# Keeping transposed rows in DRAM, and transposing heads' results by blocks on VectorE

## The chip, the cores and the metric

One core of a Trainium2 chip runs the kernel. The metric is the device time of one execution in microseconds (us), measured by the host several times; one further execution was recorded by the hardware profiler. The engines are TensorE (PE; its weight loads are listed as PEld), VectorE (DVE), ScalarE (ACT), GpSimd (POOL) and SyncE (SP), which here does nothing but issue transfers (DMAs). Each engine works through its own instructions strictly in order.

## What is computed

A transformer block on x of 8 rows (batch) x 512 tokens x 128 features, all in float32. Attention and a mixture of experts both start from the normalized input, and both are added to x:

```python
xn = _layernorm(x)                                # over the 128 features
# attention: 8 heads; each head has two score maps of 8 features
scores = einsum('bqhif,bkhif->ibhqk', xn @ Wq.T, xn @ Wk.T) * 8**-0.5
atts = softmax(scores); att = atts[0] - diff_weight * atts[1]
o = einsum('bhqk,bkhe->bqhe', att, xn @ Wv.T)
normed = o * rsqrt(mean(o * o) + eps) * norm_w    # mean over all heads of a token
attn = (normed @ Wo.T + bo) * (1 - diff_weight)
# experts: one shared and 8 routed, two of them per token
gates = sigmoid(xn @ Wg); vals, idx = top_k(gates, 2); vals /= vals.sum()
shared = silu(xn @ Ws1) * (xn @ Ws3) @ Ws2
routed = sum of vals * (silu(xn @ We1[e]) * (xn @ We3[e]) @ We2[e]) over the two experts
x + attn + (shared + routed) / 3
```

## The kernel before

Tokens lie on the 128 partitions, four tiles of 128 tokens to a row of the batch (`NT = 4`). The attention is the backbone. A row has four pairs of heads (`w`), and each pair is done in four steps (`c`, 128 keys each): 16 steps to a row, 128 in all (`STEPS * B`), numbered 0 to 127 in this text. A step has two halves. Each half issues two score matmuls (`scores`, L807, tile `sc`, a PSUM buffer with no second copy) whose exponential ScalarE takes (`pe`, L815), and two matmuls `mx` with a VectorE reduction `most` (`maxima`, L758 and L765). The maxima are those of later heads, some six steps ahead; when a pair's are complete, `shift` turns them (VectorE transposes 128x32 into `rows`, a store to `turned` in DRAM, and half a step later a load into `qst`), so that the exponentials of that pair are safe. The second half of a step also weighs the values with the exponentials of the step before (`weigh`, L826, tile `av`).

All other work is cut into pieces, which are Python generators put on a list by `job(first, last, pieces, part, ready, kept_off)`. In the first half of each step `pieces` walks the list, ordered by `last` less the pieces left, and starts the next piece of every job that fits: a piece yields a pair of its estimated TensorE time and its PSUM banks, a step has room for 3.6 us (`ROOM`) and three banks. What a job does on TensorE is issued in the first half, after that half's scores and maxima; what follows a `yield "soon"` right after the pieces of that step, and what follows `yield "late"` in the second half. So the planner fixes the order of each engine's instructions when the kernel is built. A piece of cost zero takes no room.

The jobs that matter here:

- `gates_later`: for rows 1 to 7, one a step from step 4, transposes the normalized row (`turn`, four TensorE transposes `px` into PSUM, L246), copies it out as `xnT` on ScalarE (L283) and, a step later, multiplies it by the gate weights. The pool of `xnT` has three buffers, so a row's transposed form does not stay.
- `route`: sorts tokens to experts on VectorE in steps 11 to 19. Rows are then scattered to `slots` by GpSimd, one indirect transfer a half (L441).
- `prepare(b)`: some 16 steps ahead of row `b`, transposes the row again (L665, copy L667) unless `state[b]` holds it (rows 0 and 1), makes queries and keys (`pq`, L672) and values (`pv`, L716); the parts go to `qst` and `kst` by transfers on SP (`copies`).
- `shared_ahead(b)`: the shared expert of rows 1 to 7, steps 13 to 47; transposes the row a third time (L932, copy L934) where it is not held, then `ps` (L847), tanh and two VectorE products `th_s` and `h_s`, and `ph` (L864).
- `expert(q)`, 18 groups of four blocks from step 49, one every 3.95 steps: `pxq` (transposes, L543), `ph` (L567) twice, each with a tanh on ScalarE and VectorE's `th` (L531) and `h` (L534), then `py` (L580), which needs both `h`.
- `fold(b, w)`: transposes the weighed values of a pair of heads (`po`, L876); VectorE divides (`rec` L881, `on` L883), GpSimd subtracts the second map and writes `o` (L887).
- `conclude(b)`: when the four folds of a row are done, transposes its results `o` (`pn`, L899), takes them out of PSUM scaled by `nw_s` as `oT` (L902), squares and sums them on VectorE (`sq`, L907), raises to the power -1/2 on GpSimd (L910), multiplies by Wo (`pz`, L915) and adds to the residual (`r`, four VectorE operations, L919). `kept_off` keeps its pieces out of every fourth step.

`keep_busy` and `keep_clock` are matmuls whose result is not used; in steps 0 to 3 (`CATCH_UP`) a second tile of maxima is done per step, in two separate halves (L742, L749). SP's queue carries nearly all transfers in the order of issue.

Of the kernel before, what the change touches and what calls it, by code (L numbers as in the profile page):

```python
# [19 lines left out]
P = 128  # L20
# [11 lines left out]
def kernel(  # L32
# [209 lines left out]
    def turn(b):  # L242
# [4 lines left out]
        xnT = p3.tile([P, S], F32, tag="xnT", name=f"xnT_{b}")  # L247
        return xnT, px

    gated = []  # L250
    pgs = []

# [15 lines left out]
    def gates_later(rows):  # L268

        previous = None  # L270
        for b, ready_at in rows.items():
            while step < ready_at:
                yield 0, 0
            yield 1.35, 1
            if previous:
                gates(*previous)
            if b in state and "xnT" in state[b]:
                previous = b, state[b]["xnT"]
                continue
            xnT, px = turn(b)  # L280
            previous = b, xnT
            yield "late"
            nc.scalar.copy(xnT, px)  # L283
        yield 0.9, 0
        gates(*previous)
        yield "late"
        nc.scalar.activation(
            gate.rearrange("p t e -> p (t e)"), pgs[0][:, : TILES * NE], AF.Exp, scale=-1.0
        )
        held.pop()  # L290
        gated.append(True)
# [188 lines left out]
    def keep_expert(e):  # L480
# [6 lines left out]
            in_=We2[e].rearrange("(c p) d -> p c d", p=P),  # L487
        )

    def fetch(q):  # L490

        xq = p3.tile([P, QUAD, SENT], F32, tag="xq", name=f"xq_{q}")
        ws = []
        blocks[q] = xq, ws

        def take():
            nc.sync.dma_start(
                out=xq,
                in_=slots[q * QUAD * P : (q + 1) * QUAD * P, :].rearrange("(n p) e -> p n e", p=P),
            )  # L500
            landing.append(turns + 3)

        def load(n):
            w = p12.tile([P, WIDE], F32, tag="w", name=f"w_{q}_{n}")
            j = q * QUAD + n
            e = nc.values_load(
                expert_of[0:1, j : j + 1],
                engines=[mybir.EngineType.SP],
                min_val=0,
                max_val=NE - 1,  # L510
                skip_runtime_bounds_check_because="a count of NE - 1 comparisons",
            )
            nc.sync.dma_start(out=w, in_=experts[bass.ds(e * P, P), :])
            ws.append(w)
            if n == QUAD - 1:
                fetched.append(q)
                (loads if routed else waiting).append(take)

        yield 0, 0
        yield "late"  # L520
        for n in range(0, QUAD, 2):
            loads.append(lambda n=n: (load(n), load(n + 1)))
# [137 lines left out]
    def prepare(b):  # L660

        st = state[b]
        if "xnT" not in st:
            yield 0.45, 1
            st["xnT"], px = turn(b)  # L665
            yield "late"
            nc.scalar.copy(st["xnT"], px)  # L667
        xnT = st["xnT"]
        yield 1.75, 2
        pqs = [small_psum(f"pq_{b}_{i}") for i in range(2)]  # L670
        for i in range(2):
            nc.tensor.matmul(  # L672
                pqs[i],
                w_c[:, i].rearrange("p i f u -> p (i f u)") if b else w_rest[:, i],
                xnT,
                start=True,
                stop=True,
            )
        parts = []
        for i in range(2):  # L680
            yield ("soon", "late")[i]
            upper = p1.tile([P, S], F32R, tag=f"upper{i}", name=f"upper_{b}_{i}")
            nc.scalar.copy(upper, pqs[i])
            lower = p1.tile([P, S], F32R, tag=f"lower{i}", name=f"lower_{b}_{i}")
            nc.vector.tensor_tensor(lower, pqs[i], upper.bitcast(F32), ALU.subtract)
            parts.append((upper, lower))
        q, k = qst[b % 2], kst[b % 2]

        def no_shift():
            for half in range(2):  # L690
                nc.sync.dma_start(
                    out=q[64 * half + SHIFT : 64 * half + SHIFT + 2]
                    .bitcast(F32)
                    .rearrange("p u s -> p (u s)"),
                    in_=noughts,
                )

        def copy(part, i, s):

            row_of = (2 * part + s, part + 2 * s)[i]  # L700
            first = 0 if b else 2
            for half in range(2):
                (nc.scalar if b == 0 and i and part else nc.sync).dma_start(
                    out=(q, k)[i][64 * half + row_of : 64 * half + STACK : 4, first:, :].bitcast(F32),
                    in_=parts[i][part][64 * half : 64 * half + F * (H - first), :].bitcast(F32),
                )

        if b > 1:
            copies.append(no_shift)
        for part, i in ((0, 0), (0, 1), (1, 0), (1, 1)):  # L710
            for s in range(2):
                copies.append(lambda part=part, i=i, s=s: copy(part, i, s))
        yield 0.9, 1
        pv = small_psum(f"pv_{b}")
        for t in range(NT):
            nc.tensor.matmul(  # L716
                pv[:, t * P : (t + 1) * P],
                xnT[:, t * P : (t + 1) * P],
                w_t[:, 0, :],
                start=True,  # L720
                stop=True,
            )
        yield "late"
        nc.scalar.copy(
            vals[b % 2].rearrange("p t h e -> p (t h) e")[:, :, 0:DH],
            pv.rearrange("p (n e) -> p n e", e=DH),
        )
# [52 lines left out]
    def into_queries(b, w, rows):  # L780
        n = rows.shape[0]
        for i in range(2):
            (nc.sync if b or w else nc.scalar).dma_start(
                out=qst[b % 2][64 * i + SHIFT : 64 * i + SHIFT + 2, 2 * w : 2 * w + 2, :].bitcast(F32),
                in_=rows[n // 2 * i : n // 2 * (i + 1), :],
            )
# [80 lines left out]
    def fold(b, w):  # L867
# [21 lines left out]
        )  # L889
        st["folds"] = st.get("folds", 0) + 1  # L890

    def conclude(b):

        st = state[b]
        yield 0.45, 1
        o = st["o"].rearrange("p t h e -> p t (h e)")
        pn = small_psum(f"pn_{b}")
        for t in range(NT):
            nc.tensor.transpose(pn[:, t * P : (t + 1) * P], o[:, t, :], ident)  # L899
        yield "soon"  # L900
        oT = p1.tile([P, S], F32, tag="oT", name=f"oT_{b}")
        nc.scalar.activation(oT, pn, AF.Identity, scale=nw_s)  # L902
        yield "late"
        sq = p2.tile([P, 4 * NT, DH], F32, tag="on", name=f"sq_{b}").rearrange("p n e -> p (n e)")[:, :E]
        rms = p2.tile([P, NT], F32, tag="rms", name=f"rms_{b}")
        for t in range(NT):
            nc.vector.tensor_tensor_reduce(  # L907
                sq, o[:, t, :], o[:, t, :], 1.0 / E, RMS_EPS, ALU.mult, ALU.add, rms[:, t : t + 1]
            )
        nc.gpsimd.tensor_tensor(rms, rms, minus_half, ALU.pow)  # L910
        yield 0.9, 1
        pz = small_psum(f"pz_{b}")
        for t in range(NT):
            ts = slice(t * P, (t + 1) * P)
            nc.tensor.matmul(pz[:, ts], oT[:, ts], w_t[:, 1, :], start=True, stop=True)  # L915
        yield "late"
        r = st["r"]
        for t in range(NT):
            nc.vector.scalar_tensor_tensor(  # L919
                r[:, t, :], pz[:, t * P : (t + 1) * P], rms[:, t : t + 1], r[:, t, :], ALU.mult, ALU.add  # L920
            )
        settle(b)
# [4 lines left out]
    def shared_ahead(b):  # L927

        xnT = state[b].get("xnT")
        if xnT is None:  # L930
            yield 0.45, 1
            xnT, px = turn(b)  # L932
            yield "late"
            nc.scalar.copy(xnT, px)  # L934
        hs = yield from shared_up(b, xnT)
        yield 1.8, 1
        ph = shared_down(b, hs)
# [55 lines left out]
    for b in range(B):  # L993
        at = STEPS * b
        st = state[b]
        if b == 1:
            job(1, 2, 2, prepare(b))
        elif b > 1:
            job(at - 16, at - 15, 3, prepare(b))
        if b < AHEAD:  # L1000
            job(at + 5, at + 13, 2, shared(b), lambda b=b: len(over) == b)
            job(at + 12, at + 18, 1, shared_out(b), lambda st=st: "h" in st and "r" in st)
        else:
            n = int(13 + 5.3 * (b - AHEAD))
            job(n, n + 5, 4, shared_ahead(b), lambda b=b: len(done_ahead) == b - AHEAD)
        job(
            at + 3, at + 4, 1, residual(b), lambda b=b: len(rows_sent) >= b and (b < AHEAD or b in kept)
        )
        for w in range(4):
# [3 lines left out]
        job(  # L1013
            at + 17,
            at + 21,
            2,
            conclude(b),
            lambda st=st: st.get("folds") == 4 and "r" in st,
            kept_off=b < B - 1,
# [63 lines left out]
    with tc.manual_schedule():  # L1083
# [116 lines left out]
        nc.vector.tensor_scalar(keep, dw, -1.0, 1.0, ALU.mult, ALU.add)  # L1200
        nw_s = const.tile([P, 1], F32, name="nw_s")
        nc.vector.tensor_scalar(nw_s, nw, keep, None, ALU.mult)
        nc.gpsimd.tensor_scalar(bo_b, bo_b, keep, None, ALU.mult)
        nc.gpsimd.tensor_scalar(s2, s2, OUT_SCALE, None, ALU.mult)
        count_up()
# [39 lines left out]
        while step < total + 1 or jobs or errands or loads:  # L1245
            for second_half in range(2):
# [28 lines left out]
                else:  # L1275
                    follow(begun, "late")
                    if last is not None:
                        weigh(*last)
                    if turns in CATCH_UP:
                        apart.append(True)  # L1280
                        next_maxima(1)
                        apart.pop()
# [50 lines left out]
```

## Time and profile before

| | us |
|---|---|
| median of 9 runs | 664.42 |
| lowest and highest | 659.71, 668.34 |
| the profiled execution, as timed | 659.84 |
| its span, first to last instruction | 657.7 |
| busy in the span: PE, PEld | 604.4, 313.6 |
| busy in the span: DVE, ACT, POOL | 492.9, 362.9, 288.6 |

Busy time counts an engine's instructions and not the register or DMA-issuing ones. Overlapping matmuls are counted once in a group's busy time, so a group's busy time divided by its count is less than the mean duration of one. The mean granted TensorE clock was 0.986 of full speed. A line of the timeline has the start in us from the span's start, the duration, the engine and line, the operation with the tile it writes and the tiles it reads, and in brackets how long the engine was idle before it and what ended that.

### The profile page before, as it was taken

To read this page: it belongs to the slowest core of one execution; us is meant where nothing else is said; L and a number is where in the kernel's file an instruction comes from. 1 tells how busy PE (TensorE), PEld (TensorE's weight loads), DVE (VectorE), ACT (ScalarE), POOL (GpSimd) and SP (SyncE) were. 2 spreads that over 40 slices of the span, in tenths; PEclk is the share of its full clock that TensorE was granted. 3 is DMA by queue.
4 is the path that set the end of the run, shared out by engine and by line. 5 is a ranking of instruction groups with operands and counts; after the bars stand their busy time and mean duration, and the time that the engine had idled before them with its cause. 6 is when DMAs were issued, how large, how long until landed. Compare 5 with 4: busy or idle time off the path is not lost.

```text
span 657.7 us, 10907 instructions
## 1 busy us (share of the span) xinstructions
PE 604.4 (92%) x3725; PEld 313.6 (48%) x3725; DVE 492.9 (75%) x914; ACT 362.9 (55%) x447; POOL 288.6 (44%) x488
## 2 busy tenths in 40 slices
PE   5898988889998998999999999999999999999984
PEld 2334543433443433456464655646465565646432
DVE  7768779987776775778777878778777887778633
ACT  2243554545566565655656566575566656565552
POOL 7825811036766586213506053342606333255434
PEclk9898999999999998999999999999899999999999
DMA  6353264054512331232734458323654448231075
GB/s 174 91 155 116 71 184 125 16 175 121 177 45 84 108 104 51 68 94 97 237 116 141 123 153 270 100 86 104 224 175 139 125 124 261 89 119 33 13 217 173
DMA packets 76256, 83.53 MB, mean 127 GB/s; under 512 B 11125, under 2 KB 54806, under 8 KB 76178
## 3 DMA queue, kind: packets, MB, share of 16 engines
q1 hardware_dynamic: 70246, 72.74, 36.1%
q0 software_dynamic: 4352, 9.05, 4.2%
q10 hardware_dynamic: 1604, 1.07, 0.6%
q8 instruction: 29, 0.48, 0.3%
q14 instruction: 25, 0.20, 0.1%
HBM read 48.17 MB, written 21.53 MB: 106 GB/s over the span
## 4 chain that ended last, share of the span: by engine, by line
PE 70%; DVE 16%; DMA 5%; ACT 4%; issue 3%; POOL 1%; SPq 1%; another core or an unknown queue 1%; ACTq 0%; DVEq 0%; POOLq 0%
PE sc L807 13%; PE av L826 13%; PE mx L758 11%; PE ph L567 10%; DVE most L765 8%; PE py L580 5%; PE ps L847 4%; ACT pe L815 3%; DMA ym<-results 2%; PE ph L864 2%; PE pq L672 2%; PE po L876 2%; PE pxq L543 1%; PE pg L259 1%; PE pz L915 1%
## 5 line engine op out<-in xcount | busy, mean ns | idle before, releaser
L765 DVE TENSOR_REDUCE most<-mx 128x2 f32<-128x1024 f32 x252 | 307.5, 1221 | 105.2 <-PE mx L758 98.4
L815 ACT ACTIVATE pe<-sc 128x1024 f32<-128x1024 f32 x256 | 262.5, 1025 | 217.0 <-PE sc L807 188.1
L807 PE MATMUL sc<-qst,kst 64*128 64x512 f32 x512 | 129.6, 499 | 16.2 <-ACT pe L815 13.2
L826 PE MATMUL av<-pe,vals 128*32 128x512 f32 x1024 | 138.1, 612 | 0.0
L758 PE MATMUL mx<-kst,qst 64*128 64x512 f32 x504 | 118.7, 460 | 9.3 <-DVE most L765 6.8
L807 PEld LDWEIGHTS sc<-qst,kst 64*128 64x128 f32 x512 | 48.5, 184 | 159.4 <-ACT pe L815 112.0
L1263 POOL COPY mark<-most 1x2 f32<-1x2 f32 x127 | 22.5, 178 | 159.5 <-DVE most L765 155.1
L596 POOL DMA_INDIRECT results<-y,results_at x72 | 70.9, 985 | 23.9 <-issue 17.6
L758 PEld LDWEIGHTS mx<-kst,qst 64*128 64x128 f32 x504 | 48.8, 185 | 49.6 <-DVE most L765 35.8
L441 POOL DMA_INDIRECT slots<-xn,place x64 | 63.1, 987 | 20.8 <-issue 18.4
L567 PE MATMUL ph<-xT,w 128*128 128x128 f32 x576 | 72.2, 279 | 0.0
L567 PEld LDWEIGHTS ph<-xT,w 128*128 128x128 f32 x576 | 67.1, 192 | 4.9 <-issue 4.6
L887 POOL TENSOR_TENSOR o<-on 128x128 f32<-128x128 f32 x32 | 14.8, 462 | 60.7 <-DVE on L883 60.3
L826 PEld LDWEIGHTS av<-pe,vals 128*32 128x32 f32 x1024 | 20.4, 108 | 42.3 <-issue 42.2
L580 PE MATMUL py<-w,h 128*128 128x128 f32 x288 | 38.4, 283 | 2.2 <-DVE h L534 2.2
L580 PEld LDWEIGHTS py<-w,h 128*128 128x128 f32 x288 | 33.9, 191 | 7.5 <-issue 4.2
L531 DVE SCALAR_TENSOR_TENSOR th<-th,ph 128x512 f32<-128x512 f32 x36 | 24.7, 687 | 14.4 <-ACT th L530 13.0
L530 ACT ACTIVATE th<-ph 128x512 f32<-128x512 f32 x36 | 21.5, 597 | 23.3 <-PE ph L567 22.1
L847 PE MATMUL ps<-xnT,s 128*128 128x512 f32 x64 | 32.8, 636 | 1.7 <-DVE h_s L534 1.7
L836 ACT ACTIVATE ov<-av,sides 128x512 f32<-128x512 f32 x32 | 22.3, 696 | 5.5 <-PE av L826 5.3
L534 DVE TENSOR_TENSOR h<-th,ph 128x512 f32<-128x512 f32 x36 | 24.2, 672 | 0.0
L226 POOL TENSOR_SCALAR xn<-xn,both,rstd 128x128 f32<-128x128 f32 x28 | 22.0, 798 | 0.8
(168 smaller groups left out, 592.3 us busy)
## 6 DMA issues: line engine op xcount, KB each, us to landing
w<-experts SPq DMA_DIRECT2D x72, 384.0 KB
slots<-fill SPq DMA_DIRECT2D x18, 264.0 KB
xq<-slots SPq DMA_DIRECT2D x18, 264.0 KB
ym<-results SPq DMA_DIRECT2D x16, 256.0 KB
qst<-upper SPq DMA_DIRECT2D x28, 128.0 KB
kst<-upper SPq DMA_DIRECT2D x28, 128.0 KB
qst<-lower SPq DMA_DIRECT2D x28, 128.0 KB
kst<-lower SPq DMA_DIRECT2D x28, 128.0 KB
```

Source lines behind the costliest of these rows:

```text
L441: nc.gpsimd.indirect_dma_start(out=views[TOP_K * i + k], out_offset=bass.IndirectOffsetOnAxis(ap=place[:, k, i : i + 1], axis=0), in_=sent ...
L531: nc.vector.scalar_tensor_tensor(th, th, 1.0, ph, ALU.add, ALU.mult)
L534: nc.vector.tensor_tensor(h, th, pl, ALU.mult)
L567: nc.tensor.matmul(ph[:, ns], ws[n][:, f : f + P], xT[:, ns], start=True, stop=True)
L580: nc.tensor.matmul(py[:, ns], hs[c][:, ns], ws[n][:, f : f + E], start=(c == 0), stop=(c == NF - 1))
L596: nc.gpsimd.indirect_dma_start(out=results_of[j], out_offset=bass.IndirectOffsetOnAxis(ap=results_at[:, j : j + 1], axis=0), in_=y[:, n, : ...
L758: nc.tensor.matmul(sc[:, i, :], q[ROWS[i], 2 * w + u, t * P : (t + 1) * P], k[ROWS[i], 2 * w + u, :], start=True, stop=True,)
L765: nc.vector.tensor_reduce(most[:, t, u, :], sc, AX.X, ALU.max, negate=True)
L807: nc.tensor.matmul(sc[:, i, :], kst[b % 2][ROWS[i], 2 * w + u, c * P : (c + 1) * P], qst[b % 2][ROWS[i], 2 * w + u, :], start=True, stop=True,
L815: nc.scalar.activation(pe, sc, AF.Exp, scale=F**-0.5)
L826: nc.tensor.matmul(st["av"][32 * g : 32 * g + 32, :], vals[b % 2][:, c, 2 * w + u, :], pes[u][:, i, :], start=(c == 0), stop=(c == NT - 1),)
L847: nc.tensor.matmul(ph, w[:, c * P : (c + 1) * P], xnT, start=True, stop=True)
```

## The change

Five edits:

1. `gates_later` stores each transposed row to `rows_turned` in DRAM (`keep_turned`); `prepare` and `shared_ahead` load it from there (`turned_row`) where they transposed it again. Both jobs get a piece more and start a step earlier.
2. `conclude`, for all rows but the last, stores `o` to `heads` in DRAM and loads it back in blocks of 32x32 (`in_blocks`: four loads, 512 runs of 128 bytes each) so that one VectorE transpose, which turns 32x32 blocks, gives `oT`. The job has five pieces in place of two, and the squares, the transpose and `pz` come in later steps. The last row still uses TensorE.
3. The scale `nw_s` is multiplied into the weights `w_t` once, so that `oT` is a plain copy.
4. The first two transfers of a shift move from ScalarE's queue to SP's.
5. `keep_busy` is called once more in each of steps 0 to 3.

```diff
+    rows_turned = dram.tile([B, P, S], F32, name="rows_turned")
+
+    def keep_turned(b, xnT):
+        if "xnT" not in state[b]:
+            nc.sync.dma_start(out=rows_turned[b], in_=xnT)
+
+    def turned_row(b):
+        xnT = p3.tile([P, S], F32, tag="xnT", name=f"xnT_{b}")
+        nc.sync.dma_start(out=xnT, in_=rows_turned[b])
+        yield 0, 0
+        return xnT
...
             if previous:
+                keep_turned(*previous)
                 gates(*previous)
...
+    def in_blocks(out, rows, half):
+        for i in range(2 * half, 2 * half + 2):
+            some = slice(32 * i, 32 * i + 32)
+            nc.sync.dma_start(
+                out=out[some, :].rearrange("r (n e) -> r n e", e=32),
+                in_=rows[:, some].rearrange("(n r) e -> r n e", r=32),
+            )
...
         if "xnT" not in st:
-            yield 0.45, 1
-            st["xnT"], px = turn(b)
+            yield 0, 0
             yield "late"
-            nc.scalar.copy(st["xnT"], px)
+            st["xnT"] = yield from turned_row(b)
...
-            (nc.sync if b or w else nc.scalar).dma_start(
+            nc.sync.dma_start(
...
+    heads = dram.tile([B, S, E], F32, name="heads")
+
     def conclude(b):
         st = state[b]
-        yield 0.45, 1
         o = st["o"].rearrange("p t h e -> p t (h e)")
-        pn = small_psum(f"pn_{b}")
-        for t in range(NT):
-            nc.tensor.transpose(pn[:, t * P : (t + 1) * P], o[:, t, :], ident)
-        yield "soon"
-        oT = p1.tile([P, S], F32, tag="oT", name=f"oT_{b}")
-        nc.scalar.activation(oT, pn, AF.Identity, scale=nw_s)
+        if b == B - 1:
+            yield 0.45, 1
+            pn = small_psum(f"pn_{b}")
+            for t in range(NT):
+                nc.tensor.transpose(pn[:, t * P : (t + 1) * P], o[:, t, :], ident)
+            yield "soon"
+            oT = p1.tile([P, S], F32, tag="oT", name=f"oT_{b}")
+            nc.scalar.copy(oT, pn)
+        else:
+            yield 0, 0
+            yield "soon"
+            nc.sync.dma_start(out=heads[b].rearrange("(t p) e -> p t e", p=P), in_=o)
+            yield 0, 0
+            yield "soon"
+            placed = p1.tile([P, S], F32, tag="placed", name=f"placed_{b}")
+            for half in range(2):
+                in_blocks(placed, heads[b], half)
+            yield 0, 0
         yield "late"
...
         nc.gpsimd.tensor_tensor(rms, rms, minus_half, ALU.pow)
+        if b < B - 1:
+            yield 0, 0
+            yield "late"
+            oT = p1.tile([P, S], F32, tag="oT", name=f"oT_{b}")
+            nc.vector.transpose(oT, placed)
         yield 0.9, 1
...
         if xnT is None:
-            yield 0.45, 1
-            xnT, px = turn(b)
+            yield 0, 0
             yield "late"
-            nc.scalar.copy(xnT, px)
+            xnT = yield from turned_row(b)
...
-            job(at - 16, at - 15, 3, prepare(b))
+            job(at - 17, at - 15, 4, prepare(b))
...
-            job(n, n + 5, 4, shared_ahead(b), lambda b=b: len(done_ahead) == b - AHEAD)
+            early_by = b > AHEAD
+            job(n - early_by, n + 5, 4 + early_by, shared_ahead(b),
+                lambda b=b: len(done_ahead) == b - AHEAD)
...
             at + 17,
             at + 21,
-            2,
+            5 if b < B - 1 else 2,
             conclude(b),
...
+        nc.vector.tensor_scalar(w_t[:, 1, :], w_t[:, 1, :], nw_s, None, ALU.mult)
...
                     if turns in CATCH_UP:
+                        keep_busy()
                         apart.append(True)
```

More of the change, by code (lines that the diff above doesn't have):

```diff
@@ L284, in gates_later @@
         yield 0.9, 0
+        keep_turned(*previous)
         gates(*previous)
@@ L1004 @@
             n = int(13 + 5.3 * (b - AHEAD))
-            job(n, n + 5, 4, shared_ahead(b), lambda b=b: len(done_ahead) == b - AHEAD)
+            early_by = b > AHEAD
+            job(
+                n - early_by,
+                n + 5,
+                4 + early_by,
+                shared_ahead(b),
+                lambda b=b: len(done_ahead) == b - AHEAD,
+            )
         job(
```

## The prediction

> **What bounds the kernel now.** I read the page's busy shares and chain first, then the timeline of some steps, then the waits. A "half" is the time from the start of one pair of score matmuls (`sc`) to the next, a "step" is two halves (0 to 127, sixteen to a row of the batch); halves below are differences of two `sc` starts in the timeline.
>
> ```profile
> PE 604.4 (92%) x3725; PEld 313.6 (48%) x3725; DVE 492.9 (75%) x914; ACT 362.9 (55%) x447; POOL 288.6 (44%) x488
> PE 70%; DVE 16%; DMA 5%; ACT 4%; issue 3%; POOL 1%; SPq 1%; another core or an unknown queue 1%; ACTq 0%; DVEq 0%; POOLq 0%
> ```
>
> TensorE is the bound, but not everywhere: a half with little job work cannot fall below 1.68 us (score pair 0.50, exponential 1.02 and two hand-overs; the single `sc` buffer forces that loop). Read so, the first half of a step lasts 1.70 with `pxq` alone, 2.73 with `ps`, 2.80 with `ph`, 3.22 with `ph` and `pxq`, 4.57 with `py` and `ph`, 3.20 with `po` and `ph`. Job work is thus paid in full only above some 1.1 us, and VectorE enters where TensorE waits for `h`:
>
> ```profile
> 345.72 1.23 DVE most L765
> 346.95 0.17 DVE rec L881
> ...
> 347.14 0.42 DVE on L883
> 347.57 0.61 DVE h L534
> ...
> 348.22 1.83 PE py L580 x14
> ```
>
> That is the chain in step 63: `py` starts the moment that VectorE, working strictly in order, has done `most`, `rec`, `on` and `h`. The half lasts 3.35 us, against 2.79 for `py` in step 56, where no `rec` and `on` stand before `h`.
>
> **What the change removes.** Transposes `px`: 76 take 12.7 us, 19 sets of four; 8 sets stay, 11 go: 11 x 0.67 = 7.4 us of TensorE, and 11 copies of 0.58 on ScalarE. `pn`: 7 of 8 sets go, 7 x 0.64 = 4.5 us, with 7 evacuations of 0.69. Together 11.8 us of TensorE. With `pn` goes its wait for GpSimd's `o`:
>
> ```profile
> PE pn L899 <- POOL o L887: 6.6, 5, 1.9
> ```
>
> and, in one case, a slow clock behind it (columns: window, length, busy of PE, PEld, DVE, ACT, POOL, clock, DMA):
>
> ```profile
> 211.40:215.40 4.00, 3.90 (x8) 1.37 (x8) 0.69 (x1) 1.28 (x2) 1.14 (x3) 0.59 0.55 159
> ```
>
> That step (35) had a first half of 6.36 us where `ps` alone takes 2.73.
>
> **What it adds.** Four `keep_busy` matmul pairs in steps 0 to 3, 9.6/13 = 0.74 us each: 0 to 3.0 us; VectorE ends those halves (two or three reductions each), so I take 0.5. Seven VectorE transposes of 128x512: the trace has only 128x32 at 0.21 us; bounds 0.21 and sixteen times that, 3.4; I take 0.68, what the SBUF and PSUM passes over 128x512 take (`h`, L534). The scale on `w_t` is one small operation in the start-up. And 52 DMAs on SP: 6 stores and 11 loads of turned rows, 7 stores of heads, 28 block loads. SP issues take 0.24 to 0.65 us in the trace, so 12 to 34 us of a queue that mostly waits; each heads store now waits there for `o`, with the copies to `qst` and `kst` behind it, which have seven steps to go. The block loads have 7 x 2048 packets of 128 bytes. The mean packet of SP's queue (36.1% of 16 engines' 657.7 us over 70,246 packets) took 54 ns: 2048 x 54 / 16 = 6.9 us a row at most, 1.0 at the best slice's 270 GB/s. They are issued in step 52 (and its like) and read by VectorE at the end of step 55, 13 us later; the turned rows are loaded at least 5 us ahead. So I cost both at nothing. If that cover went, VectorE would stand at `oT` with all maxima behind it, microsecond for microsecond. [...]
>
> **What it moves, and this decides.** With `px` and `pn` gone the planner fits other jobs into their room: steps 67 to 71 of the changed kernel hold `ph`; `ph pxq`; `py ph`; `po ph`; `py`, which is word for word what steps 75 to 79 hold in the kernel before. So the time can be read off the same trace (same columns):
>
> ```profile
> 364.26:387.14 22.88, 22.86 (x174) 15.05 (x170) 19.23 (x41) 13.32 (x17) 5.57 (x8) 1.00 0.39 116
> 400.98:424.85 23.87, 23.58 (x176) 15.62 (x172) 19.04 (x35) 13.19 (x17) 5.93 (x11) 1.00 0.50 161
> ```
>
> Steps 67 to 71 go from 22.88 to 23.87 because `py` moves in from step 72. But VectorE's order changes too: `conclude` now needs three more steps, and its four squares (`sq`, each 0.29 and a read of 0.08; 293.38 to 294.67 in the trace, 1.29 us) land in step 70 between `most` and `rec on h`, the very chain shown above. There `py` waits for `h` already, so 1.29 us is added in full: 25.16, +2.28. That such a displacement is paid is seen in steps 53 and 69, both `py pxq`: 4.20 and 3.22 us; in 53 the four `r` (1.12 us) run ahead of `h`, in 69 behind it. Steps 72 and 73 then hold only `pz`: 2.15 instead of 2.79 (it waits 0.25 for the VectorE transpose), but the four `r` fall into a step with nothing on TensorE and hold up the next maximum: 2.5 instead of 1.68 in the half after, with 1.68 instead of 1.98 before it: together -0.1. Step 64 loses `px`: -0.1.
>
> The sum, by steps:
> - 0 to 15: +0.5.
> - 18 to 21: VectorE never rests here. Followed instruction by instruction from 128.1 us, 24.7 becomes 22.0: -2.7 (bounds 0 and -5).
> - 34 to 37: `px` out -0.4, `pn` and its slow clock out -3.6, then 3.62 to 2.73 and 3.77 to 2.85: -5.8.
> - second halves after a `px` (24, 29, 33, 44, 45, 49), 1.92 to 1.96 because its copy stands before an exponential, to 1.68: -1.7.
> - `pz` and `r` of rows 0 and 1 in new places: step 26 +0.9, the half after 27 +1.2, 38 and 39 +0.8, 40 +1.1: +4.0.
> - 51 to 55: 24.51 to 25.16, +0.65; 67 to 71 and their two repeats 3 x 2.28 = +6.85; what surrounds them -0.9: +6.6.
> - 115 to 121: `pn` and `pz` leave 115 and 116 (-1.3), squares before `h` in 118 (+1.3), `pz` and `r` in 120 (+1.2): +1.3 with 0.1 of small ones.
> - the clock: TensorE waits 1.6 us for `h` in five places. After waits of 1.6 to 2.0 us the granted clock fell to 0.57 to 0.60 three times of five in this trace (the window above, and from 54.3 and 253.0 us), at some 1.5 us each. Bounds 0 and 7.5; I take +2.0.
>
> Sum +4.2 us. [...] The sum stands against the profiled execution, 659.84 us (span 657.7), which lies 4.6 below the median of 664.42; runs spread from 659.71 to 668.34. I set the sum on the median: 664.42 + 4.2 = 668.6 us.
>
> **The rivals.** Faster: the squares find VectorE idle. Place: between `most` and `h` in steps 54, 70, 86, 102, 118; if VectorE gains 1.6 us there by the copies and waits that are gone, 5 x 1.29 and the 2.0 for the clock drop out: 668.6 - 8.5 = 660, and if all 11.8 us of TensorE counted, 652.6. For it: the chain is 70% TensorE, and 22.86 of 22.88 us are busy. Against it: the row of 423 us shows `py` waiting for `h` in exactly this setting. It decides if VectorE ends `on` 1.3 us earlier than now.
>
> Even: losses and gains of some 14 us each meet within 0.5% (3.3 us), about the least that a measurement of this kernel can tell from no change. Stage 16 to 47 would have to give 3 more than I count.
>
> Much slower: SP's queue. Where the expert copies fill it, TensorE already stood 2.0 us for a shift (`qst<-turned`, 96.6 us), with the shift's row having only some 10 us from maximum to use. If the added transfers make five such waits of the eleven shifts in steps 4 to 47: +10, 679 us. Against it: DMA engines are 30% busy there on average.
>
> That the change does not do what it says I leave out: the changed order shows the 44 and 28 transposes gone.
>
> **How the numbers follow.** Forecast (slower by some 4) 0.34, SP's queue 0.15, even 0.25, faster 0.26. Alone the forecast has 664 to 674. For 8 in 10 the range takes in the faster case but its far end and the queue's: 655 to 680. Faster than 661.1 0.26; between 0.25; slower than 667.7 0.49.
>
> **What would show it.** Right: in the waits, `py` for `h` far above its 5.5 us (loads and matmuls), steps 67 to 71 about 25 us; no `pn` wait; step 35 near 2.7 us. Wrong: steps 67 to 71 at 23.9 or less, waits of VectorE for the block loads or of `sc` for `turned`, or a VectorE transpose far from 0.7 us.

## The result and the profile after

The changed kernel takes 679.33 us (median of 20 runs, 674.77 to 690.34), the kernel before, in 62 runs beside them, 663.97 (656.76 to 671.72). The ratio is 1.0252, 95% interval 1.0227 to 1.0276: slower by 15 to 18 us, where +4.2 was forecast. The two profiled executions differ by more, 683.99 against 659.84 us: the one of before lay 4 us below its median, the one of after 5 above. (Ratios, and the means of clock and time below, leave disturbed runs out.)

The page of the changed kernel, busy shares and chain:

```profile
PE 614.5 (90%) x3661; PEld 315.8 (46%) x3661; DVE 498.5 (73%) x922; ACT 354.0 (52%) x429; POOL 287.7 (42%) x488
PE 65%; DVE 17%; DMA 7%; issue 4%; ACT 2%; SPq 2%; POOL 2%; another core or an unknown queue 0%; DVEq 0%; ACTq 0%
```

TensorE does 64 matmuls fewer and is busy 10 us longer: what is left runs at a lower clock (0.959 on average, against 0.986). Its part of the chain is 65% where it was 70%; DMA rose from 5% to 7%. In its list of waits (total, times, longest) the turned rows' transfers are new, the copy `xnT` waiting for a row's store and `ps` for a row's load, and the waits of `py` for `h` (loads and matmuls) grew from 5.5 us to 17.8:

```profile
ACT xnT L297 <- DMA rows_turned<-xnT: 10.0, 3, 4.2
PE ps L870 <- DMA xnT<-rows_turned: 2.9, 1, 2.9
PEld py L604 <- DVE h L558: 9.6, 7, 1.7
PE py L604 <- DVE h L558: 8.2, 7, 1.5
```

I followed the start of every half in both traces. The table says how much later than in the kernel before each stage makes the changed kernel (profiled executions, us), beside the forecast's terms put into the same stages:

| steps | forecast | changed kernel |
|---|---|---|
| start to 7 | +0.5 | +2.8 |
| 7, 8 | 0 | +9.2 |
| 9 to 15 | 0 | -0.6 |
| 16 to 21 | -2.7 | -2.8 |
| 22 to 25 | -0.3 | +6.0 |
| 26 to 33 | +1.5 | +1.6 |
| 34 to 37 | -5.8 | -5.5 |
| 38 to 47 | +1.3 | +2.0 |
| 48 to 121 | +9.6 | +11.2 |

Three stages are off: the start, steps 7 and 8, and steps 22 to 25. The start is no finding: over the kernels below it lies anywhere from -2 to +5, whatever their edits there. The other two are waits for the turned rows' transfers. The table has a flaw in its base: the profile of the kernel before ran at a clock of 0.89 in steps 42 to 44 and lost 2.8 us there, and another 1.4 to 1.7 from step 48 on, that the profiles of runs 13 and 14 below, whose code is the same there, did not lose. Against those two the last two rows would read +4.8 and about +12.8.

Steps 7 and 8, timeline (start, duration, engine, line; in brackets the idle time before it and what ended it):

```profile
76.27 0.41 SPq L254 DMA_DIRECT2D rows_turned<-xnT  x1
79.08 0.58 ACT L297 COPY xnT<-px 128x512 f32<-128x512 f32 x1 [4.12 <-DMA rows_turned<-xnT]
79.72 1.87 PE L272 MATMUL pg<-wg,xnT 128*128 128x8 f32 x8 [2.95 <-ACT xnT L297]
...
83.81 0.93 SPq L237 DMA_DIRECT2D slots<-fill  x2
84.84 0.49 SPq L254 DMA_DIRECT2D rows_turned<-xnT  x1
...
88.55 0.59 ACT L297 COPY xnT<-px 128x512 f32<-128x512 f32 x1 [4.21 <-DMA rows_turned<-xnT]
```

The same two copies in the kernel before wait for nothing:

```profile
76.84 0.58 ACT L283 COPY xnT<-px 128x512 f32<-128x512 f32 x1
81.67 0.58 ACT L283 COPY xnT<-px 128x512 f32<-128x512 f32 x1
```

The store of a row is issued in the same piece that transposes the next one, and the next one's copy follows in the same step. Of the three `xnT` buffers, two hold rows 0 and 1 until `ps` has read them in steps 14 and 19, so the copy must write the very buffer that the store is still reading: 2.8 us from the store's issue to the copy's start, and 3.7 in step 8, where the store was also issued behind the fills. The first halves take 6.60 and 4.53 us instead of 2.31 twice, and the granted clock is 0.66 over those 13 us (the window 79.08 to 92.00).

Step 24:

```profile
166.54 1.86 SPq L509 DMA_DIRECT2D placed<-heads  x4
168.46 1.29 SPq L726 DMA_DIRECT2D qst<-lower  x2
169.79 0.46 SPq L259 DMA_DIRECT2D xnT<-rows_turned  x1
...
174.37 2.93 PE L870 MATMUL ps<-xnT,s 128*128 128x512 f32 x4 [2.85 <-DMA xnT<-rows_turned]
```

The row's load stands on SP behind the block loads of edit 2 and a part of the queries; TensorE has it 4.6 us after issue. Before, `px` made the row in step 23, and `ps` did not wait:

```profile
161.28 1.98 PE L847 MATMUL ps<-xnT,s 128*128 128x512 f32 x4
```

Steps 67 to 71, the place that the forecast rested on (window without the last half, as the prediction's was):

```profile
376.72:402.94 26.22, 24.70 (x176) 16.64 (x172) 19.67 (x39) 13.03 (x16) 7.39 (x10) 0.95 0.53 149
```

26.22 against 25.16 forecast, with a clock of 0.95. Step 71 itself has the forecast's chain, operation by operation:

```profile
396.35 1.23 DVE L788 TENSOR_REDUCE most<-mx 128x2 f32<-128x1024 f32 x1 [0.25 <-PE mx L781]
397.49 0.28 DVE L944 CUSTOM_DVE_ANT_0 sq<-o 128x128 f32<-128x128 f32 x1
...
398.70 0.25 DVE L904 RECIPROCAL rec<-po 128x16 f32<-128x16 f32 x1
398.99 0.42 DVE L906 TENSOR_TENSOR on<-po,rec 128x256 f32<-128x256 f32 x1
399.33 0.68 DVE L558 TENSOR_TENSOR h<-th,ph 128x512 f32<-128x512 f32 x1
400.06 2.95 PE L604 MATMUL py<-w,h 128*128 128x128 f32 x14 [1.52 <-DVE h L558]
```

The squares run from 397.49 to `rec`, 1.2 us, and `py` waits. But `py`'s 14 matmuls take 2.95 us instead of 1.83, at a clock of 0.59 (400.06 to 402.94). And step 35 lost its `pn` and its slow clock:

```profile
227.26:230.01 2.75, 2.75 (x18) 0.83 (x16) 2.27 (x3) 1.31 (x3) 1.51 (x4) 1.00 0.68 207
405.31 0.70 DVE L952 STREAM_TRANSPOSE oT<-placed 128x512 f32<-128x512 f32 x1
```

2.74 us from `sc` to `sc` (6.36 before, 2.73 forecast); the VectorE transpose took 0.70 (0.68 forecast).

### The profile page after: what moved, and what is told of

It is laid out like the page before. It is cut to its first block, busy times and chain, and to the rows that moved or that the text cites. A ratio compares the mean times of both kernels' runs of the same rounds, so it can differ in the third digit from the quotient of the medians.

```text
span 682.2 us, 10847 instructions
## 1 busy us (share of the span) xinstructions
PE 614.5 (90%) x3661; PEld 315.8 (46%) x3661; DVE 498.5 (73%) x922; ACT 354.0 (52%) x429; POOL 287.7 (42%) x488
## 2 busy tenths in 40 slices
DMA packets 97185, 91.67 MB, mean 134 GB/s; under 512 B 26293, under 2 KB 73558, under 8 KB 97106
## 4 chain that ended last, share of the span: by engine, by line
PE 65%; DVE 17%; DMA 7%; issue 4%; ACT 2%; SPq 2%; POOL 2%; another core or an unknown queue 0%; DVEq 0%; ACTq 0%
PE av L849 12%; PE sc L830 11%; PE mx L781 10%; PE ph L591 10%; DVE most L788 8%; PE py L604 5%; PE ps L870 4%; DMA ym<-results 2%; PE pq L695 2%; ACT pe L838 2%; PE ph L887 2%; DMA kst<-lower 2%; PE po L899 2%; PE pz L957 1%; PE pg L1262 1%
## 5 line engine op out<-in xcount | busy, mean ns | idle before, releaser
L830 PE MATMUL sc<-qst,kst 64*128 64x512 f32 x512 | 131.4, 507 | 19.1 <-ACT pe L838 12.3
L849 PE MATMUL av<-pe,vals 128*32 128x512 f32 x1024 | 140.2, 621 | 0.0
L781 PE MATMUL mx<-kst,qst 64*128 64x512 f32 x504 | 120.7, 471 | 11.9 <-DVE most L788 9.4
L604 PE MATMUL py<-w,h 128*128 128x128 f32 x288 | 43.9, 306 | 9.1 <-DVE h L558 8.2
L604 PEld LDWEIGHTS py<-w,h 128*128 128x128 f32 x288 | 38.1, 209 | 15.4 <-DVE h L558 9.6
```

Of the source, the lines that this page charges most:

```text
L604: nc.tensor.matmul(py[:, ns], hs[c][:, ns], ws[n][:, f : f + E], start=(c == 0), stop=(c == NF - 1))
L781: nc.tensor.matmul(sc[:, i, :], q[ROWS[i], 2 * w + u, t * P : (t + 1) * P], k[ROWS[i], 2 * w + u, :], start=True, stop=True,)
L830: nc.tensor.matmul(sc[:, i, :], kst[b % 2][ROWS[i], 2 * w + u, c * P : (c + 1) * P], qst[b % 2][ROWS[i], 2 * w + u, :], start=True, stop=True,
L849: nc.tensor.matmul(st["av"][32 * g : 32 * g + 32, :], vals[b % 2][:, c, 2 * w + u, :], pes[u][:, i, :], start=(c == 0), stop=(c == NT - 1),)
```

## The experiments

My theory from this profile: the missing 11 us are the rows' store holding the buffer (A), and the late row; the squares' place (B) costs what was forecast, and more where the clock falls. Rivals: the added transfers cost by filling SP's queue wherever they stand; the waits only move time that another wait gives back; the clock falls for other reasons. Ratios are to runs of the kernel before made beside each kernel; "stage" numbers are profiles against the profile of before, as in the table above.

**1. Other buffers for the gates' rows.**

```diff
-            xnT, px = turn(b)
+            px = small_psum(f"px_{b}")        # and the four transposes
+            xnT = p3.tile([P, QUAD, SENT], F32, tag="xq", name=f"xnT_{b}")
+            xnT = xnT.rearrange("p n s -> p (n s)")[:, :S]
```

> Edit: the turned rows 2 to 7 of the gates take the three idle buffers of the tag xq instead of the one buffer of the tag xnT that is left to them (rows 0 and 1 hold the other two); nothing else changes. Theory A (in steps 7 and 8 ScalarE's copy waited 4.1 us and 4.2 us for the store to rows_turned that still had to read that buffer, and the store stood behind other transfers on SP): steps 7 and 8 go back to about what they take in the kernel before, some 9 us less than in the changed kernel's profile; ratio to the kernel before about 1.012 instead of 1.0252, and no wait of the xnT copy for rows_turned over 0.5 us. Rival (the stores' place in SP's queue itself delays the shifts and the fills, and the slow clock there comes from that; the buffer is only where it shows): steps 7 and 8 keep at least 6 of the 9 us, the wait shows at another line (slots, qst or kst), ratio 1.021 or more.

Measured: 1.0187 (1.0087 to 1.0288), which holds both sides' ratios. Steps 7 and 8 take what they took before (+0.0), and no such wait is left but one of 1.23 us at 85.5. But steps 9 to 15 now lose 5.7, where the changed kernel lost none:

```profile
96.77 0.98 PE L834 MATMUL sc<-qst,kst 64*128 64x512 f32 x2 [2.96 <-DMA qst<-turned]
```

This is the wait for a shift that the kernel before has at step 11 (2.04 us there). The kernels below that lose 9 us or more in steps 7 and 8 find the shift landed at step 11, so a part of the 9 us can be given back. It is not always: in runs 2 and 9 the clock stayed low after the loss (0.58 in steps 9 to 11), and steps 9 to 15 lost 4.9 us as well.

**2. `first_rows` issued by ScalarE again.**

```diff
-            nc.sync.dma_start(
+            (nc.sync if b or w else nc.scalar).dma_start(
```

> Edit: the two transfers of first_rows are issued by ScalarE again, as in the kernel before; all else as changed. Theory (behind four issues on SP they came 1.5 us late at the first sc, and the slow start clock went on longer): the first sc starts 1.5 us earlier after its shift, steps 0 to 2 give back 1.5 to 4 us, ratio about 1.020 to 1.023. Rival (the first steps are set by the maxima on VectorE and by the cold clock, so an earlier first sc only waits later): ratio 1.025, offset at step 4 still above 3 us.

Measured: 1.0281 (1.0166 to 1.0395). The first `sc` came earlier, but so it did in runs 1 and 3, which do not have this edit; at step 4 the offset was +2.4. No effect can be told from the scatter of the start, so the theory is not supported; nor is it refuted, since the interval holds its ratio too.

**3. Squares in the step of the heads' store.**

```diff
             nc.sync.dma_start(out=heads[b]..., in_=o)
+            yield "late"
+            squares()      # sq and rms, as they stood behind the block loads
             yield 0, 0
```

> Edit: the four squares of conclude run two or three steps earlier, in the step that stores the heads (before the h of a ph step), instead of between most and rec, on, h in the step of py; TensorE's order is unchanged. Theory B (py waits for h behind the squares, 1.29 us in each of steps 55, 71, 87, 103 and 119, and the wait makes the clock fall behind it): those first halves go from 4.57 to 6.07 us to 3.2 to 3.6 us, with the clock at 1.00 in the second halves, 8 to 11 us in all; ratio about 1.011. Rival (VectorE is full over the whole row, so that 1.29 us comes back in whatever step holds the squares): first halves of 52, 68, 84, 100, 116 grow by 1 us or more each, and only the clock's part, 3 to 5 us, is gained; ratio 1.018 to 1.021.

Measured: 1.0120 (1.0013 to 1.0228). All five first halves take 3.35 or 3.36 and the halves after them 1.67 or 1.68; the first halves of steps 52, 68, 84 and 100 stay at 3.22 or 3.23. Steps 48 to 121: -0.5 instead of +11.2. In step 71:

```profile
397.35 0.25 DVE L904 RECIPROCAL rec<-po 128x16 f32<-128x16 f32 x1
397.63 0.42 DVE L906 TENSOR_TENSOR on<-po,rec 128x256 f32<-128x256 f32 x1
397.97 0.68 DVE L558 TENSOR_TENSOR h<-th,ph 128x512 f32<-128x512 f32 x1
398.70 1.83 PE L604 MATMUL py<-w,h 128*128 128x128 f32 x14 [0.30 <-DVE h L558]
```

`rec` follows `most` at once and TensorE waits 0.30 instead of 1.52. The rival falls: VectorE has room for the squares two steps earlier.

**4. The three edits together.**

> Edit: the three edits together (other buffers for the gates' turned rows, first_rows issued by ScalarE, squares in the step of the heads' store). If the causes are separate places of the kernel, their gains add: 9 + 2.5 + 9 = some 20 us less than the changed kernel, ratio about 0.995. Rival (one bound, such as VectorE or the clock, takes the place of each): less than 14 us, ratio 1.004 or more.

Measured: 1.0051 (0.9994 to 1.0107), 13 us less than the changed kernel (1.0252 - 1.0051, of 664). That is the rival's number: the gains do not add up to the 20 us of the theory. What is left in its profile: +5.7 in steps 9 to 15 (the shift, as in 1), +3.8 in 22 to 25 and +3.6 in 38 to 47.

**5. The row's load sooner.**

```diff
         hs = yield from shared_up(b, xnT)
+        if b + 1 < B:
+            fetch_row(b + 1)      # the load of turned_row, on SP
         yield 1.8, 1
```

> Edit: the three edits of the run before, and the load of the next turned row for the shared expert is issued as soon as the row before has given its h, one to two steps earlier than now and ahead of the block loads on SP. Theory (in step 24 ps waits 2 to 3 us for a row whose load was issued behind the four block loads and a shift's transfers, and the clock falls around it): steps 23 and 24 go back to 1.7, 2.0, 2.7 and 1.7 us, some 4 us less than with the three edits alone; ratio about 0.999. Rival (the row's load only pushes the placed blocks and the shifts back by the same time, the DMA engines being at 0.86 of their time there): steps 22 to 27 together shorter by less than 1.5 us, ratio 1.004 or more.

Measured: 1.0008 (0.9958 to 1.0057). The load that was issued at 166.36 in run 4 now goes at 146.31; steps 23 and 24 take 1.68, 1.96, 2.75 and 1.67, as before the change to 0.01. In the six profiles of the whole change without this edit (after, 1 to 4 and 15) steps 23 and 24 are together 3.8 to 7.3 us longer than in the kernel before, in the three with it (5, 11 and 12) 0.0. Not all of that need be the row: in the heads-only kernels below, which load no row, these steps are 1.1 to 2.2 us longer too.

**6 to 10. The two halves of the change alone.** The rows through DRAM (run 6: with the buffers of 1, heads as before), and the heads in blocks (run 7: squares early, rows turned by TensorE as before), both without edits 4 and 5:

> The first half of the change alone: turned rows through DRAM (with the other buffers for the gates' rows), heads concluded as in the kernel before, no further keep_busy. Theory (the 11 px sets save what the steps after them show, 0.25 us each with 0.4 in step 34 and some 2.5 in steps 16 to 20, and lose 4 us in step 24 where the row lands late and some 3 us in steps 11 to 14 where the stores stand ahead of a shift): 0 to +3 us against the kernel before, ratio 1.000 to 1.005. Rival (7.4 us of TensorE are worth their time): ratio 0.990. Rival (the added SP transfers cost more than that): 1.010.

> The second half of the change alone: heads through DRAM in blocks and VectorE's transposes, with the squares in the step of the heads' store; the rows are turned by TensorE as in the kernel before, no further keep_busy. Theory (with the squares out of the way the conclusion costs nothing in steps 51 to 119 and saves 5 us in steps 35 to 37, less 4 us for pz and r of rows 0 and 1 in their new steps): -2 to 0 us against the kernel before, ratio 0.997 to 1.000. Rival (the heads' and block transfers stand ahead of shifts on SP): a wait of sc for turned, ratio 1.006 or more.

Rows alone: 1.0169 (1.0096 to 1.0241), slower than the theory and both rivals had it. Heads alone: **0.9889 (0.9842 to 0.9937)**, 654.18 us against 661.63, better than its theory: the version that beats both kernels. It waits 4.12 us for the shift at step 11 and gains 3.4 us in steps 16 to 21 and 5.4 in 34 to 37. The rows-only kernel keeps `pn`, and has +0.4 and -1.7 in those stages: the gains of steps 16 to 21 and 34 to 37 belong mostly to the heads' half. The 11 sets of `px` that it drops, 7.4 us of TensorE, gave nothing: in ten of the eleven steps that held one (16, 28, 32, 34, 39, 44, 48, 64, 80 and 96) it takes the same time as run 13, which still has them, to 0.02 us; in the eleventh, 23, it is slower. In step 28 the second `sc` waits for the exponential with `px` ahead of it (kernel before) and without (rows alone):

```profile
179.94 0.50 PE L807 MATMUL sc<-qst,kst 64*128 64x512 f32 x2 [0.22 <-ACT pe L815]
191.06 0.51 PE L834 MATMUL sc<-qst,kst 64*128 64x512 f32 x2 [0.80 <-ACT pe L842]
```

Then heads with late squares (run 8) and rows with the old buffer (run 9), each as the change has it, and rows with sooner loads (run 10):

> The second half of the change alone, as in the heads-only run, but with the squares where the change puts them (in the step of py, ahead of rec, on and h). Theory (the place of the squares costs the same without the turned rows): 9 to 11 us more than the heads-only run, ratio about 1.003 to 1.006, first halves of steps 55, 71, 87, 103 and 119 at 4.6 us or more. Rival (the squares only cost as much as they do because VectorE runs late for other reasons, those of the turned rows): less than 4 us more, ratio 0.995 or less.

> The first half of the change alone, with the gates' rows in the one xnT buffer, as the change has them. Theory (the copy's wait for the store costs 9 us in steps 7 and 8, and hides a wait for a shift at step 11 that every kernel pays that comes there on time, 4 us): 5 us more than the rows-only run with the other buffers, ratio 1.022 to 1.027. Rival (the time given up in steps 7 and 8 is all given back by step 14): ratio 1.018 or less.

> The first half of the change alone, with the other buffers and with the row loads of the shared expert issued one to two steps earlier. Theory (the late row costs 2 to 3 us in step 24; the remaining loss of the rows-only run lies in pn of rows 0 and 1, which now waits for o in steps 20 and 35): 2 to 3 us less than the rows-only run, ratio about 1.013. Rival (earlier loads push other transfers back by as much): ratio 1.017 or more. If the 7.4 us of px count after all once no row is late: 1.000 or less.

Late squares: 1.0002 (0.9964 to 1.0039), 0.0113 more than with early ones, 7.5 us, between theory and rival. Its profile has all five waits and the clock at 1.00 in each:

```profile
385.23 1.83 PE L589 MATMUL py<-w,h 128*128 128x128 f32 x14 [1.51 <-DVE h L543]
```

Old buffer: 1.0171 (1.0120 to 1.0221) in four runs. The ratio is that of run 6, on the rival's side, but not for its reason: in the profile steps 7 and 8 lose 9.8 us and nothing is given back by step 15 (+4.9 there, +4.6 in run 6). Inconclusive. Sooner loads: 1.0069 (1.0036 to 1.0101), below the theory's 1.013. Steps 22 to 25 are +2.5 us with them and without, so the late row was not there. It was in step 40 of the rows-only kernel:

```profile
247.55 3.42 PE L874 MATMUL ps<-xnT,s 128*128 128x512 f32 x4 [1.86 <-DMA xnT<-rows_turned]
```

That first half took 6.11 us (5.60 with the old buffer) and takes 2.74 with sooner loads, as before the change. The mechanism held, and its place moves with what else stands on SP. The stage as a whole did not show it (steps 38 to 47 +1.7 us, +0.7 without sooner loads), since the clock was 0.74 in steps 42 to 44 of that execution.

**11. Stores from ScalarE's queue** (`nc.scalar.dma_start(out=rows_turned[b], ...)`, with run 5).

> Edit: as the run with the earlier row loads, and the six stores of the turned rows are issued by ScalarE instead of SP. Theory (at step 11 sc waits 2.8 us for a shift, 0.8 more than in the kernel before, since a store of 0.55 us stands ahead of it on SP; the clock falls to 0.50 behind it and steps 12 to 14 lose 3.7 us more): the wait at step 11 goes to 2.0 us or less, steps 11 to 14 take 4 us less than in that run. Rival (the shift waits for the transfers of the expert weights, which are as many as before; ScalarE's issues delay the exponentials): steps 11 to 14 unchanged within 1 us.

Measured: 1.0127 (1.0053 to 1.0201), against 1.0008 in run 5. The theory missed: `sc` waited 4.77 us at step 11, and 2.90 us at step 8, a wait no other kernel had. The rival's steps 11 to 14 came out (0.8 us more than in run 5), but not by its reason. The order on SP is that of run 5 without the stores; what differs is that SP itself stood still. Its own list of waits has six for the stores that ScalarE issued (L730 is the line of the queries' and keys' transfers, L237 that of the fills), which no other kernel's list has; the third line is the wait at step 8:

```profile
SPq L730 <- DMA rows_turned<-xnT: 13.1, 3, 8.1
SPq L237 <- DMA rows_turned<-xnT: 10.5, 3, 3.8
85.39 0.59 PE L834 MATMUL sc<-qst,kst 64*128 64x512 f32 x2 [2.90 <-DMA qst<-turned]
```

SP issued the two shifts at 81.78 and 107.48 us, where run 5 did at 73.93 and 99.31. Why transfers on SP wait for stores of another queue is not shown. It is the forecast's third rival in small: behind transfers that waited up to 8.1 us, SP issued these shifts 7.9 and 8.2 us later than in run 5.

**12. All of it mended, without the four added `keep_busy`.**

> All of the change with its three places mended and the earlier row loads, and without the four added keep_busy. Theory (keep_busy lies beside VectorE's reductions): within 0.3% of the run with them, ratio 0.998 to 1.004. Rival (the four pairs, 3.0 us of TensorE, come in full and also set the clock of the start): ratio 0.996 or less, steps 0 to 4 shorter by 3 us.

Measured: 0.9967 (0.9934 to 1.0000), just below the theory's range; the interval overlaps that of run 5. `keep_busy` is worth less than can be measured.

**13 and 14. The stores alone, in the kernel before**, with its buffer and with those of run 1:

```diff
             if previous:
+                keep_turned(*previous)      # stored, and read by nobody
                 gates(*previous)
```

> Edit: the kernel before with one addition: the six stores of the turned rows 2 to 7 to DRAM, as the change has them; nothing reads them, and all rows are still turned by TensorE. Theory (the stores hold the single free xnT buffer): steps 7 and 8 lose 9 us and the shift's wait at step 11 goes, 2 to 5 us in all; ratio 1.005 to 1.010, by the profile 5 us or more. Rival (stores on an otherwise waiting queue are free, as the forecast had it): steps 7 and 8 as before, ratio 0.998 to 1.002.

> Edit: as the run of the kernel before with the stores, but the six rows take the three idle xq buffers. Theory: steps 7 and 8 as in the kernel before, the wait at step 11 present; ratio 0.998 to 1.003. Rival (the stores cost by their place on SP): the shift at step 11 later by 0.5 us per store ahead of it, ratio 1.005 or more.

Measured: 1.0101 (1.0059 to 1.0143) and 0.9995 (0.9962 to 1.0027). This is the price of A: 0.0106, 7.0 us, by one buffer; six stores on SP as such cost nothing that can be measured. The profile of the first:

```profile
74.50 0.58 ACT L290 COPY xnT<-px 128x512 f32<-128x512 f32 x1 [4.25 <-DMA rows_turned<-xnT]
83.82 0.58 ACT L290 COPY xnT<-px 128x512 f32<-128x512 f32 x1 [4.07 <-DMA rows_turned<-xnT]
```

Steps 7 and 8 +10.3, then -1.7 to step 15.

**15 and 16. TensorE's idle time ahead of `h` filled**, in the changed kernel and in the heads-only kernel with late squares:

```diff
         py = small_psum(f"py_{q}")
+        if step > 50 and step % 16 == 7:
+            for _ in range(2):
+                nc.tensor.matmul(py[:, : 2 * P], ident, s1[:, :], start=True, stop=True)
```

> Edit: the changed kernel, but in steps 55, 71, 87, 103 and 119 two 128x256 matmuls on constants (0.70 us each) are put ahead of py on TensorE; the first real py overwrites them. VectorE's order, and so the time at which h is ready, is unchanged. Theory (it is TensorE's idle 1.5 us before h that lets the clock fall behind it): the clock stays at 1.00, the five first halves take 4.57 to 4.75 us, the halves after them 1.68, and steps 48 to 121 lose 5 to 6 us against the kernel before instead of 11; ratio 1.015 to 1.020. Rival (the clock falls by the state of the whole kernel, not by this wait; the heads-only run with late squares waited as long and kept its clock): first halves of 5.2 us and more again, ratio 1.025.

> Edit: the heads-only run with the late squares, with two 128x256 matmuls on constants ahead of py in steps 55, 71, 87, 103 and 119. Theory (the five idle times of 1.5 us on TensorE cost clock in most executions: the run without them had a mean clock of 0.976 against 0.985 with early squares): mean clock 0.982 or more, ratio 0.993 to 0.997, some 3 to 4 us less than without the matmuls. Rival (the clock depends on something else, such as VectorE's work or the start): mean clock 0.976 to 0.978, ratio 0.999 to 1.002.

Measured: 1.0261 (1.0209 to 1.0313) and 1.0007 (0.9969 to 1.0044), so no gain in time in either. In the profiles the clock does what the theory says: the ten first halves take 4.56 or 4.57, and steps 67 to 71 of the changed kernel read

```profile
377.25:402.33 25.08, 24.43 (x180) 16.39 (x177) 19.67 (x39) 13.04 (x16) 6.27 (x9) 1.00 0.52 148
```

against 25.16 forecast. Without the fill the clock fell in 8 of 20 such steps (4 of 5 in the changed kernel, to a mean of 0.78 over each of the steps 71, 87, 103 and 119; 3 in run 1, 1 in run 2, none in run 8). But the mean clock over the runs is 0.967 with the fill and 0.966 without, and 0.979 with and without in the heads-only pair: what these steps keep is too little to see. Steps 48 to 121 cost 5.1 us in both filled kernels, and in run 8, whose clock held without the fill: that is the squares' place without the clock (6.5 to 6.9 against the profiles of runs 13 and 14).

## Why the prediction was wrong

It was right on the side, and the range held; the size was off by 11 us, above all because two terms were set at nothing.

- **The six stores of turned rows, without a term in the sum**: the step that failed. I priced the transfers on SP and the DMA engines, where they cost nothing that can be measured (run 14, 0.9995), and did not ask who must wait until a store has read its source. The description of the kernel before had it: three `xnT` buffers, a copy a step. Measured 7.0 us in the kernel before (runs 13 and 14), 9.2 in the changed kernel's profile. In the changed kernel the ratio fell by 0.0065 with other buffers (run 1), with overlapping intervals, and between runs 6 and 9 no difference shows.
- **"The turned rows are loaded at least 5 us ahead"**, also at nothing: I read the order of pieces, not the queue. In step 24 the load was issued 4.6 us ahead of use and behind the block loads of the same change. 3.8 to 7.3 us in profiles (run 5); the ratio fell by 0.004, with overlapping intervals.
- **Squares before `h`**: right in mechanism, place and price. 1.22 us in each of five steps (4.57 with late squares, 3.35 with early ones; 25.08 in steps 67 to 71 once the clock is held). Early squares take all of it back. Whole stage, steps 48 to 121: 5.1 us without the clock, where the forecast had 7.6.
- **The clock**: +2.0, bounds 0 to 7.5. In the profile the steps from 48 on lost some 6 that way (11.2 - 5.1); over the runs, the mean clock is 0.966 against 0.979. Within both kernels a lower mean clock goes with a longer time, 5.0 us for each 0.01 in 20 runs of the changed one and 5.4 in 78 of the one before; by that, some 7 of the 16.7 us between the two means (679.3 and 662.6) go with the clock, and some 10 do not. That the waits for `h` alone cause it is not shown, since filling them did not shorten the runs. Waits of 1.5 us were followed by a fall 8 times in 20, so my three of five is not a price.
- **Steps 16 to 21 and 34 to 37**: -2.8 and -5.5 against -2.7 and -5.8. Read off the same trace's rows, they came out to a few tenths, and they came again in the kernels whose code is the same there (runs 1, 2 and 15: -2.6 to -3.2, -5.5 to -5.8). In step 35 the long first half behind `pn` (6.36 us in the kernel before, its clock 0.59 from 211.4 to 215.4 us) was no accident: it came again, 6.65 and 6.11 us, in runs 13 and 14, whose code is the same there. It is not `pn` alone: the rows-only kernels keep `pn`, and take 4.96 or 4.97 us there at a clock of 1.00.
- **The moved `pz` and `r`**: +1.6 in steps 26 to 33 against +1.5 is luck in part, since runs 1, 2 and 15, with the same code there, have +1.6, +3.1 and +5.1. So is +2.0 against +1.3 in steps 38 to 47: steps 38 to 40 lost 4.6 us where 1.6 was forecast, and the kernel before's own slow stretch in steps 42 to 44 gave 2.8 back.
- **Second halves after a `px`, -1.7**: a wrong reading. The sets stand in steps 23, 28, 32, 39, 44 and 48 (the forecast's step numbers are off), and without `px` and its copy the second halves of 28, 32, 44 and 48 still take 1.92 to 1.95 us. What sets them is not the copy: in step 28 of the changed kernel `most` ends at 196.54, `mx` starts at 196.60, `av` at 197.02, and the next `sc` behind it at 198.02.
- **Block loads at nothing**: right. No wait of VectorE for `placed` in any list, with 26,293 packets under 512 bytes instead of 11,125. The only cost of the small ones that showed is the 1.86 us of issue of four block loads in front of the row's load (step 24).
- **The third rival** (SP's queue, +10): nearest in size to what came, for another reason. No shift was late in the changed kernel; a buffer and a row were.

Open: why the rows' half stays slower than the kernel before (1.0069) with both its waits mended; what the 2.5 us are that the rows-only kernels, and run 8, lose in steps 22 to 25, where none of their matmuls waits for a row; and how much of the clock the waits cost.

## What to carry over

The stores to DRAM were not free where their source buffer was about to be written again (7.0 us in the kernel before, and nothing that can be measured with other buffers): ask of each added transfer not only which queue and engine it takes, but which buffer it holds, and until when, and count buffers that others hold for long. A load moved onto SP's queue was late by what stood ahead of it there (1.86 and 1.29 us of issues ahead of the row for which `ps` then waited 2.85 us in step 24), not by its position in the schedule; the step that reads it decides. When a change has halves, price them apart: here one half, with four operations moved, gave 1.1%, and the other took it and more. And work taken off the busiest engine saved nothing in steps that waited for something else: here eleven sets of `px`, 7.4 us of TensorE.

## What the runs showed that I had not expected

- Removing 7.4 us of TensorE work (11 sets of `px`) shortened, in the rows-only kernel, none of the steps that held it: in step 28 `px` stood where TensorE waits for the exponential anyway, 0.8 us without it.
- Eleven kernels that came on time through steps 7 and 8 wait 1.3 to 4.1 us for a shift at step 11, the kernel before among them (2.0); the six that lost 9 us or more there find the shift landed.
- The same program's mean clock differs from run to run (0.955 to 0.974 over 20 runs of the changed kernel), and its time with it (684.0 to 674.8 us from the longest to the shortest).
